# A Mamba and mixture-of-experts layer on one core: expert features spread over the partitions by copies, one DMA per routing weight tile, and a planner with free buffers and one DMA queue

## The chip, the core and the metric

The kernel runs on one core of one Trainium2 chip. The metric is device time in microseconds, the median of several runs. The core has TensorE (PE, matrix products), VectorE (DVE), ScalarE (ACT), GpSimd (POOL) and SyncE (SP, which here issues DMAs). Each engine executes its own queue of instructions in order and waits on semaphores for the others. Sixteen DMA engines move data between the device memory (DRAM) and the on-chip memories: SBUF, and PSUM, into which TensorE writes. Both have 128 partitions.

## What is computed

The input is 16 batches of 256 positions with 256 features, all in 32-bit floats. Each is normalised, and two branches read the result; the output is the input plus both.

```python
xn = layernorm(x)
# branch 1: a selective state space (Mamba) layer, E = 512 features, N = 16 states
hidden, gate = split(xn @ W_in)                  # 256 -> 2 * 512
hidden = silu(causal_conv4(hidden) + conv_bias)
dt, Bm, Cm = split(hidden @ W_x, [128, 144])
dts = softplus(dt @ W_dt + b_dt)
dA  = exp(dts[..., None] * -exp(A_log))          # 512 x 16 per position
dBu = dts[..., None] * Bm[:, :, None, :] * hidden[..., None]
state = dA * state + dBu ; y = sum_n state * Cm  # a scan over the 256 positions
out1 = ((y + hidden * D) * silu(gate)) @ W_out
# branch 2: 32 experts of 96 features each, the best 8 of a token weighted
probs = softmax(xn @ router_w.T); w = top8(probs) / sum(top8(probs))
out2 = sum_e ((silu(xn @ w_gate[e]) * (xn @ w_up[e])) @ w_down[e]) * w[:, e]
x + out1 + out2
```

All 32 experts are computed for every token; an expert that is not among a token's eight has weight zero.

## The kernel before

The work is cut into steps (small functions such as `project`, `feed`, `scan`), each on one engine. At the end of `mamba_moe_kernel` every step of every batch is handed to a planner with `add(...)` (from line 816): its engine, a length, a due time, the steps it `needs`, the buffers it `takes` and those it `gives` back. `Plan.order` (line 56) plays all of it through once at build time: whenever an engine is free, the ready step with the earliest due time starts. The order found is the order in which the instructions are issued; nothing is reordered on the chip. A due time is a base (`ORIGIN + PERIOD * b` for the Mamba steps, `ORIGIN + RATE * b + LEAD` for the experts) plus an offset per kind of step from the table `DUE`, and from `FIRST`, `SECOND` and `LAST` for the first, second and last batch. `EARLY` says how long ahead of its due time a step may start. Many offsets are thousands of microseconds, so they act as fixed ranks between kinds of steps.

Buffers of a kind form a ring of a size from `RINGS` (line 260). `open` (line 49) lets a step start when the next buffer in turn is free, and `take` (line 266) hands the buffers out strictly in turn. A DMA is modelled as a length on its issuing engine and a fixed time `lands` until its data is there; transfers do not delay one another in the model.

**Mamba branch.** `load_x`, `stats`, `root`, `invert`, `center` (two POOL instructions, line 403) and `norm` normalise; `turn` and `keep_turned` transpose to `xnT`. `project` (line 556, bank kinds g and u), `conv_first` and `conv_rest`, and `activate` make `hs`; `params`, `lift`, `turn_steps`, `widen`, `steps` make `dts`; `send_params` writes Bm and Cm to DRAM (`bcd`). `inputs` (POOL) multiplies. Then come 8 groups of 2 states: `fetch` (SP, line 680) reads two rows of B and C repeated to all partitions into `rep`; `feed` (POOL, line 692) multiplies the scan's input; `decay` (ACT), `scan` and `read` (DVE) follow, and `collect` (POOL) adds the products into `y` by an accumulating DMA. `fold`, `gated` and `project_out` end the branch; `gate` and `gate_silu` make its gate.

**Expert branch.** The 32 x 96 = 3072 features are 24 chunks of 128, in 4 parts of 8 experts or 6 chunks. `load_experts` (line 323) brings the weights of a part once, at the start, and all batches use them. `route`, `largest`, `expo` and `choose` compute the routing weights, `send_weights` writes them to DRAM (`wd`). For each part, `spread` (line 492) reads them back so that partition p of chunk c holds the weight of the expert that this feature belongs to: as 96 does not divide 128, an expert's features straddle chunks, and a part takes six DMAs (line 501) into a tile `wr` of 128 x 6 x 256. For each pair q of chunks, `gates` and `ups` (line 508, L515) are matmuls, `silu` (L528) gives `sg`, `weigh` (POOL, L534) multiplies `sg` by `wr`, `combine` (DVE, L538) multiplies by the ups to `h`, and `down` (L550) accumulates into `acc`. `settle` and `finish` add the two branches to the reloaded input, and `store` writes it.

**Opening.** ACT issues five small loads of per-feature vectors into `small` (line 291), SP the larger ones. `warm` and `keep_warm` (line 372) are transposes of the identity on TensorE whose results are not used.

## Time and profile before

| | |
|---|---|
| median of 3 runs | 1309.12 us (1308.93 to 1309.49) |
| profiled execution | 1305.62 us |
| its span, first to last instruction | 1303.3 us |
| mean granted TensorE clock | 0.992 of full speed |
| instructions | 19008 |
| DMA moved | 268.80 MB, mean 206 GB/s |
| DMA issues of `rep` / `wr` / `y` from `pr` | 128 / 384 / 222 |
| median issue to landing of these | 6.7 / 6.0 to 6.4 / 7.2 us |

The page gives each engine's busy time and its share of the span, the span in 40 slices, the DMA queues, the chain of work that ended last, and groups of instructions by source line. "PE ... L515" is an instruction of TensorE that line 515 issued; "pg<-xnT,wg_sb" names what it writes and reads; `<-` ahead of an engine's name says who ended a wait. SPq and POOLq are the engines' queues, where a DMA is issued. A batch appears in the trace as one `ph` (project) pair, 24 chunks of `pg`, `pu` and `acc`, and 16 units of `bu`, `da` and `pr`.

### The profile page before, as it was taken

The numbers are of one execution on the slowest core, as the hardware profiler recorded it, in microseconds if no ns is written. First come the engines' busy times: TensorE is split into PE (matmuls) and PEld (weight loads), VectorE is DVE, ScalarE is ACT, GpSimd is POOL, SyncE is SP. The second block draws the span as 40 slices with busy tenths as digits, with TensorE's granted clock in tenths as the row PEclk, the third lists the DMA queues.
The fourth block names the chain that finished last, engine by engine and source line by source line (L and its number), as shares of the span: only waits on it lengthen the run. The fifth ranks groups of instructions, "written<-read, shape, count | busy, mean of one in ns | idle before, by whom it ended". The sixth has DMA issues, their size and how long they took to land.

```text
span 1303.3 us, 19008 instructions
## 1 busy us (share of the span) xinstructions
PE 1269.5 (97%) x6010; PEld 1111.8 (85%) x6010; DVE 1157.6 (89%) x1735; ACT 1102.1 (85%) x1888; POOL 1181.3 (91%) x835
## 2 busy tenths in 40 slices
PE   8988999999999999999999999999999999999998
PEld 7877788888888888888888888888888888888877
DVE  3778899999899999998989999889989899889887
ACT  5869898998889989798897989799888898888873
POOL 1778999999999999999999999989999899898994
PEclk8998999999999999999999999999999999999999
DMA  9999999998999989899998999989899898989994
GB/s 248 245 225 204 194 221 210 222 209 184 219 218 213 217 195 213 195 219 196 203 221 192 211 208 207 211 199 213 190 208 206 195 234 185 210 191 204 204 228 83
DMA packets 174292, 268.80 MB, mean 206 GB/s; under 512 B 42704, under 2 KB 108272, under 8 KB 174192
## 3 DMA queue, kind: packets, MB, share of 16 engines
q0 software_dynamic: 36576, 124.80, 50.8%
q1 hardware_dynamic: 134976, 142.75, 41.0%
q8 instruction: 47, 0.77, 0.2%
q10 hardware_dynamic: 2640, 0.05, 0.1%
q14 instruction: 53, 0.43, 0.1%
HBM read 137.51 MB, written 5.24 MB: 110 GB/s over the span
## 4 chain that ended last, share of the span: by engine, by line
PE 56%; POOL 19%; DMA 7%; issue 6%; ACT 6%; DVE 5%; SPq 1%; POOLq 0%; DVEq 0%; ACTq 0%
PE acc L550 15%; PE pu L515 14%; PE pg L515 14%; POOL bu L695 7%; POOL sg L534 5%; POOL y L734 4%; PE po L788 3%; DMA wr<-wd 3%; PE ph L561 3%; PE pgate L762 3%; DMA rep<-bcd 2%; ACT da L709 2%; PE px L599 2%; DVE da L717 2%; PE pdt L643 1%
## 5 line engine op out<-in xcount | busy, mean ns | idle before, releaser
L695 POOL TENSOR_TENSOR bu<-rep,hs 128x1024 f32<-128x1024 f32 x256 | 701.0, 2893 | 39.8 <-DVE da L717 20.0
L717 DVE TENSOR_TENSOR_SCAN da<-da,bu 128x512 f32<-128x512 f32 x512 | 608.8, 1216 | 38.4 <-ACT da L709 25.9
L709 ACT ACTIVATE da<-dts,a_sb 128x256 f32<-128x256 f32 x1024 | 469.2, 473 | 95.4 <-DVE pr L729 71.7
L550 PE MATMUL acc<-wd_sb,h 128*128 128x256 f32 x1536 | 364.8, 380 | 5.3 <-DVE h L538 4.8
L515 PE MATMUL pu<-xnT,wu_sb 128*128 128x256 f32 x1536 | 360.0, 380 | 7.5 <-DVE h L538 6.4
L515 PE MATMUL pg<-xnT,wg_sb 128*128 128x256 f32 x1536 | 350.1, 381 | 6.3 <-ACT sg L528 5.6
L515 PEld LDWEIGHTS pg<-xnT,wg_sb 128*128 128x128 f32 x1536 | 292.7, 191 | 48.5 <-ACT sg L528 6.8
L515 PEld LDWEIGHTS pu<-xnT,wu_sb 128*128 128x128 f32 x1536 | 290.4, 191 | 48.9 <-DVE h L538 8.5
L550 PEld LDWEIGHTS acc<-wd_sb,h 128*128 128x128 f32 x1536 | 291.6, 191 | 46.9 <-DVE h L538 6.7
L534 POOL TENSOR_TENSOR sg<-sg,wr 128x512 f32<-128x512 f32 x192 | 317.8, 1858 | 4.9 <-DMA wr<-wd 3.4
L734 POOL DMA_DIRECT2D y<-pr x222 | 289.3, 1313 | 23.0 <-DVE da L717 6.1
L729 DVE TENSOR_TENSOR pr<-da,rep 128x512 f32<-128x512 f32 x448 | 293.4, 675 | 5.4 <-issue 2.9
L538 DVE TENSOR_TENSOR h<-pu,sg 128x512 f32<-128x512 f32 x192 | 130.9, 682 | 61.9 <-POOL sg L534 36.6
L709 ACT ACT_TABLE_LOAD x135 | 173.2, 1283 | 2.4
L528 ACT ACTIVATE sg<-pg 128x512 f32<-128x512 f32 x192 | 104.7, 593 | 4.1 <-PE pg L515 1.7
L528 ACT ACT_TABLE_LOAD x81 | 103.9, 1283 | 3.5 <-PE pg L515 2.2
L584 DVE SCALAR_TENSOR_TENSOR hs<-ph,small,hs 128x255 f32<-128x255 f32 (+2 forms) x192 | 76.8, 471 | 2.9 <-ACT hs L573 2.9
L753 POOL TENSOR_TENSOR y<-y 128x512 f32<-128x512 f32 x32 | 67.6, 2233 | 2.2 <-DMA y<-pr 2.2
L561 PE MATMUL ph<-xnT,win_sb 128*128 128x256 f32 x256 | 64.1, 396 | 1.9 <-DMA win_sb<-in_L_attn_W_in_dram 1.9
L788 PE MATMUL po<-wout_sb,y 128*128 128x256 f32 x256 | 62.1, 386 | 2.9 <-POOL y L778 2.9
L762 PE MATMUL pgate<-xnT,win_sb 128*128 128x256 f32 x256 | 58.2, 380 | 2.0 <-ACT sg L528 1.9
L778 POOL TENSOR_TENSOR y<-y,gs 128x512 f32<-128x512 f32 x30 | 58.4, 2414 | 0.0
(69 smaller groups left out, 844.9 us busy)
## 6 DMA issues: line engine op xcount, KB each, us to landing
y<-pr POOLq DMA_DIRECT2D x222, 512.0 KB, 7.2
rep<-bcd SPq DMA_DIRECT2D x128, 512.0 KB, 6.7
wr<-wd SPq DMA_DIRECT2D x128, 192.0 KB, 6.0
wr<-wd SPq DMA_DIRECT2D x128, 128.0 KB, 6.4
wr<-wd SPq DMA_DIRECT2D x128, 64.0 KB, 6.0
y<-sk POOLq DMA_DIRECT2D x32, 256.0 KB, 7.2
xt<-L_attn_input_states_dram SPq DMA_DIRECT2D x16, 256.0 KB, 6.0
o<-L_attn_input_states_dram SPq DMA_DIRECT2D x16, 256.0 KB, 6.5
```

Of the source, the lines that this page charges most:

```text
L515: nc.tensor.matmul(p[:, j, :], w[:, hc, ts(c, P)], xs[:, hc, :], start=(hc == 0), stop=(hc == HC - 1),)
L528: nc.scalar.activation(sg, live.pop(("g", b, q)), AF.Silu)
L534: nc.gpsimd.tensor_mul(sg, sg, wr[:, r : r + 2, :])
L538: nc.vector.tensor_mul(h, live.pop(("u", b, q)), live.pop(("sg", b, q)))
L550: nc.tensor.matmul(acc[:, s, :], h[:, j, ts(s, P)], wd_sb[:, c, :], start=(c == 0 and s == 0), stop=(c == FC - 1), skip_group_check=True,)
L561: nc.tensor.matmul(ph[:, j, :], win_sb[:, hc, ts(2 * q + j, P)], xs[:, hc, :], start=(hc == 0), stop=(hc == HC - 1),)
L695: nc.gpsimd.tensor_mul(bu, live["rep", b, g][:, 0:1].to_broadcast([P, CPU, NG, L]), live["hs", b][:, ts(u, CPU), :].unsqueeze(2).to_broadc ...
L709: nc.scalar.activation(da[:, i, :], dts[:, c, :], AF.Exp, scale=a_sb[:, c, n : n + 1])
L717: nc.vector.tensor_tensor_scan(flat, flat, live["bu", k][:, j].rearrange("p n l -> p (n l)"), 0.0, op0=ALU.mult, op1=ALU.add,)
L729: nc.vector.tensor_mul(live["pr", k][:, :, j, :], live.pop(("da", m)), live["rep", b, g][:, 1])
L734: nc.gpsimd.dma_start(live["y", b, u].rearrange("p n c l -> p (n c l)"), live.pop(("pr", k)).rearrange("p n c l -> p (n c l)"), accum_op=A ...
L788: nc.tensor.matmul(po[:, s, :], y[:, 0, j, ts(s, P)], wout_sb[:, c, :], start=(c == 0 and s == 0), stop=(c == EC - 1), skip_group_check=True,)
```

## The change

Features are laid out anew. A part of 8 experts has 768 features; partition p now holds features 6p to 6p + 5 of the part, so 16 partitions hold one expert and all six chunks of a part have the same expert on a given partition. A routing weight tile is then 128 x 256, loaded by one DMA, and `weigh` reads it for both chunks of a pair. The down weights come in this order from one DMA of whole rows per part. Gate and up weights are loaded by the same kind of DMA as before, into one of four staging areas (the second buffers of `y0`, `y1`, `hs`, `dts`, which batch 1 is the first to use), and a VectorE copy `deal` puts them in the new order; 16 loads and 16 copies. The second batch's `project` needs the last copy.

The planner gives a step any free buffer, the one longest free (`spare`), instead of the next in turn; it keeps steps of one kind in order; it models one DMA queue through which all transfers pass one after another, and at most 8 outstanding transfers of SP. Rings: `wr` 4 for 2, `sg` 5 for 3, `h` 3 for 2. `gates` and `gate` are two steps each in place of one, with a lock that keeps a pair together. `down`-weight loads are steps of their own. The small loads are issued by POOL instead of ACT, the first batch's `center` is one VectorE instruction, its `route` comes after its first `project`, and `keep_warm` makes 20 and 8 transposes in place of 6 and 4. All offsets in the tables are new, and ORIGIN, PERIOD, RATE and LEAD are -27.68, 78.24, 79.23 and -62.04, for -13.55, 77.76, 77.96 and -22.78.

```diff
 class Plan:
+    BEGIN = dict(SP=1.3, POOL=2.0)
+    FINISH = 0.6
+    LANES = 8
...
-    def open(self, ring, count):
...
+    def transfer(self, st, now):
+        piece = st["length"] / st["parts"]
+        for _ in range(st["parts"]):
+            if st["engine"] == "SP":
+                now = max(now, self.lanes.pop(0))
+            self.busy = max(self.busy, now + self.BEGIN[st["engine"]]) + st["moves"] / st["parts"]
+            landed = self.busy + self.FINISH
+            if st["engine"] == "SP":
+                self.lanes.append(landed)
+            now += piece
+        return now, landed
+
+    def spare(self, ring):
+        return [
+            k for _, k in sorted(
+                (self.given[key], k) for k, key in enumerate(self.slots[ring]) if key in self.given
+            )
+        ]
...
-        rep=3, bu=3, pr=4, da=AHEAD, g=2, u=2, acc=1, wr=2, sg=3, h=2, gs=2, o=1,
+        rep=3, bu=3, pr=4, da=AHEAD, g=2, u=2, acc=1, stage=4, pair=1, wr=4, sg=5, h=3, gs=2, o=1,
...
-        i = taken[ring] % RINGS[ring]
-        taken[ring] += 1
+        i = plan.homes[ring].pop(0)
...
-        nc.scalar.dma_start(
+        nc.gpsimd.dma_start(
             small[:, :, 0:KC], conv_k.rearrange("(c p) o k -> p c (o k)", p=P)
...
+    STAGES = ("y0_1", "y1_1", "hs_1", "dts_1")
+
+    def load_down(j):
+        nc.sync.dma_start(
+            wd_sb[:, ts(j, CPG), :],
+            w_down[ts(j, EPG)].rearrange("e i h -> (e i) h").rearrange("(p c) h -> p c h", c=CPG),
+        )
+
+    def load_experts(j, kind, hc):
+        src = {"g": w_gate, "u": w_up}[kind]
+        home = STAGES[plan.homes["stage"].pop(0)]
+        stage = sb.tile([P, SLAB], F32, tag=home, name=f"stage_{j}_{kind}_{hc}")
+        stage = stage[:, : EPG * I].rearrange("p (e i) -> p e i", e=EPG)
+        nc.sync.dma_start(stage, src[ts(j, EPG), ts(hc, P), :].rearrange("e p i -> p e i"))
+        live["stage", j, kind, hc] = stage
+
+    def deal(j, kind, hc):
+        dst = {"g": wg_sb, "u": wu_sb}[kind]
+        stage = live.pop(("stage", j, kind, hc)).rearrange("p e i -> p (e i)")
+        nc.vector.tensor_copy(
+            dst[:, hc, ts(j, CPG), :], stage.rearrange("p (m c) -> p c m", c=CPG)
+        )
...
     def center(b):
+        if b == 0:
+            nc.vector.scalar_tensor_tensor(
+                nmr, mv[:, :, 0:1], -1.0, rstd, op0=ALU.mult, op1=ALU.mult
+            )
...
     def spread(b, g):
-        wr = take(sb, "wr", [P, CPG, L], f"wr_{b}_{g}")
-        half = EPG // 2
-        for e in range(half):
-            lo, hi = e * I, (e + 1) * I
-            while lo < hi:
-                c, r = divmod(lo, P)
-                n = min(hi - lo, P - r)
-                nc.sync.dma_start(
-                    wr[r : r + n, c :: CPG // 2, :],
-                    wd[g * EPG + e : (g + 1) * EPG : half, :].partition_broadcast(n),
-                )
-                lo += n
+        wr = take(sb, "wr", [P, L], f"wr_{b}_{g}")
+        rows = live["wd", b][ts(g, EPG), :]
+        nc.sync.dma_start(wr, rows.unsqueeze(1).to_broadcast([EPG, ROWS, L]))
...
     def weigh(b, q):
-        nc.gpsimd.tensor_mul(sg, sg, wr[:, r : r + 2, :])
+        sg, wr = live["sg", b, q], live["wr", b, 2 * q // CPG]
+        nc.gpsimd.tensor_mul(sg, sg, wr.unsqueeze(1).to_broadcast([P, 2, L]))
...
-    add("keep_warm", (1,), "PE", 1.3, -490.0, 6, needs=[("turn_router",)])
-    add("keep_warm", (2,), "PE", 0.8, -490.0, 4, needs=[("turn", 0)], gives=["warm"])
+    add("keep_warm", (1,), "PE", 2.3, -490.0, 20, needs=[("turn_router",)])
+    add("keep_warm", (2,), "PE", 0.9, -490.0, 8, needs=[("turn", 0)], gives=["warm"])
...
+            for hc in range(HC):
+                add("load_experts", (j, kind, hc), "SP", 0.6, due, j, kind, hc, moves=1.65,
+                    takes=[("stage", ("stage", j, kind, hc))])
+                add("deal", (j, kind, hc), "DVE", 0.85, due, j, kind, hc,
+                    needs=[("load_experts", j, kind, hc)], gives=[("stage", j, kind, hc)])
...
+        dealt = [("deal", PARTS - 1, "u", HC - 1)] if b == 1 else []
```

The offsets that set SP's first issues are, by kind, `DUE` plus `FIRST`: `load_again` -7024.7 - 13951.6, `load_x` -8639.1 + 792.8, `load_in` 1119.4 - 7928.7, `load_router` -358.6 - 6402.5, `load_steps` -7426.2 + 5634.6, `load_experts` -3572.6 + 1952.1, `load_out` 9300.8 - 2.6. Their base times are -27.68, -210, -199 and 20, -200, -198, -89.7 and 45. `EARLY` holds the four down loads back to about 18, 38, 57 and 77 of the planner's microseconds.

## The prediction

> **What bounds the kernel now.** I read the busy shares and slices first, then busy time by stage, then TensorE's instructions in time, then the chain of waits, then the DMA queue's own waits.
>
> ```profile
> PE 1269.5 (97%) x6010; PEld 1111.8 (85%) x6010; DVE 1157.6 (89%) x1735; ACT 1102.1 (85%) x1888; POOL 1181.3 (91%) x835
> DMA  9999999998999989899998999989899898989994
> 80.00:100.00 20.00, 16.42 (x75) 13.85 (x74) 14.60 (x22) 10.46 (x21) 15.90 (x11) 0.91 0.81 215
> 100.00:180.00 80.00, 71.59 (x332) 62.06 (x331) 69.70 (x103) 69.10 (x119) 72.61 (x52) 0.96 0.95 202
> 500.00:580.00 80.00, 80.00 (x384) 70.60 (x383) 74.55 (x111) 69.78 (x121) 73.86 (x52) 1.00 0.93 205
> ```
>
> The stage rows give length, then busy us of PE, PEld, DVE, ACT and POOL, then granted clock and DMA share. From 500 to 580 TensorE never stops: here it is the bound. Sixteen matmuls start over 3.45 us, 0.216 us each, and the same step of two batches (686.82 and 764.79 in the chain) lies 77.97 us apart. Sixteen batches are 16 x 77.97 = 1247.5 us of work that the change leaves alone, so only what TensorE loses can be won: 1303.3 - 1247.5 = 55.8 us. POOL has 1181.3 / 16 = 73.8 us a batch, DVE 72.4, ACT 68.9: little room when one of them is late.
>
> ```profile
> 8.45 1.08 PE L438 MATMUL pl<-rwT,xnT 128*128 128x32 f32 x8 [0.24 <-ACT xnT L428]
> 11.44 6.20 PE L561 MATMUL ph<-xnT,win_sb 128*128 128x256 f32 x16 [1.91 <-DMA win_sb<-in_L_attn_W_in_dram]
> 87.11 2.75 PE L550 MATMUL acc<-wd_sb,h 128*128 128x256 f32 x8 [3.16 <-DVE h L538]
> 110.86 6.00 PE L515 MATMUL pg<-xnT,wg_sb 128*128 128x256 f32 x16 [5.34 <-ACT sg L528]
> 137.62 1.99 PE L515 MATMUL pu<-xnT,wu_sb 128*128 128x256 f32 x8 [3.05 <-DVE h L538]
> ```
>
> Each row is start, length, instructions, and in brackets the idle time before it. Setting each stretch of matmuls against 0.216 us apiece gives the losses: (a) 12.8 us up to 17.47, of 17.47 us only 4.7 being work (turn 0.44, routing 0.82, project 3.45); (b) 18.5 us from there to 140: 1.7 before 28.2; 3.3, 0.6, 5.5 and 3.2 idle; and 0.8 + 1.0 + 2.4 because matmuls after the 3.16 and 5.34 us gaps ran at a granted clock of 0.50 for some 4 us; (c) 16.4 us after 140, in 17 pieces of 0.4 to 2.3, nearly 13 of them after 860; (d) 3.9 us behind the last matmul. The rest, some 4 us, is in gaps under 0.35.
>
> ```profile
> 0.74 3.22 DMA small<-_L_attn_conv_kernel_dram
> 3.98 0.37 SPq L795
> 5.46 5.84 DMA win_sb<-in_L_attn_W_in_dram
> ...
> 62.38 1.31 POOL sg L534
> 63.69 1.80 SPq L501
> 66.72 9.80 DMA wr<-wd
> 76.68 1.27 POOL sg L534
> ...
> 314.74 9.36 DMA wr<-wd
> 324.17 6.72 DMA rep<-bcd
> ```
>
> The chain (start, length, what) says why. At the start SP stands still from 2.15 until ACT's `small` load has landed, so `win_sb` is issued only at 5.46. Later, a routing weight tile comes free (`weigh`, L534), SP writes out its six DMAs (L501), they land 9.8 us later, POOL waits, and VectorE and TensorE after it: the idle at 84 to 87 follows. The same pair stands at 314, before the 1.3 us loss at 346. SP's own waits say the same:
>
> ```profile
> SPq L501 <- POOL sg L534: 129.0, 32, 10.4
> SPq L683 <- DVE pr L729: 306.4, 81, 11.1
> ```
>
> What waits behind a `wr` DMA on SP are the `rep` fetches (L683) that `feed` needs.
>
> **The change, part by part.**
>
> *Routing weights.* Now 384 DMAs (L501, median 0.599 us of SP each) carry 64 x 128 x 6 x 1 KB = 50.3 MB. After: 64 DMAs, 8.4 MB. SP is freed of 320 x 0.6 = 192 us, 12 a batch. The queue's kind carries 142.75 MB in 41.0% of the engines' time, so 41.9 MB are about 12% of it, and the mean DMA share falls from 0.93 to about 0.81. Landings (`wr` 6.1, `rep` 6.7, `y` 7.2 us median) should shorten, I take by a tenth to a quarter. `weigh` reads one row for both chunks; no POOL row has just that, but `feed` reads both operands repeated at 2.33 us for 1024 (2.28 ns each) against `weigh`'s 1.26 for 512 (2.46), so I cost it at nothing, between -0.1 and +0.1 us each, and +0.1 x 12 = 1.2 a batch stays inside POOL's 4.2 of room.
> The Trainium skill speaks against the new form: "DMA: Bandwidth & Descriptors", section Rules for kernel authors, says that an outermost dimension below 16 confines a transfer to that many engines, and this source's outermost dimension is 8. No row here shows such a transfer. By it 128 KB would take 8 engines about 1.0 us instead of 0.5 at the first slice's 248 GB/s, an estimate; the sum would not move, since four tiles give most of a batch of lead.
>
> *Deeper buffers, any free one:* `wr` 4 for 2, `sg` 5 for 3, `h` 3 for 2. This is what lets a late transfer pass: one `sg` more holds 1.73 us of matmuls, two 3.5, against stalls of 0.4 to 5.5. TensorE's order, with `gates` and `gate` split into halves of 1.73 us, can fill more holes.
>
> *Opening.* SP takes what is due first. Base time plus the tables give -21004 for the residual (256 KB), -8056 for x (256), -7008 and -6789 for the halves of `win_sb` (512 each), -6961 for the router (32). Before, x alone landed at 3.83: 0.74 for the issue, 256 KB at 248 GB/s is 1.06, so 2.0 fixed. After: x at about 4.9, `win_sb` 7.0, router 7.1 (before 4.5). From x to the turned x took 8.40 - 3.83 = 4.6 us; `center` on VectorE, one instruction of 0.2 instead of POOL's 0.62 from invert to norm, takes 0.3 off. Turned x is then due at 9.1; but the router's turn at 7.1 and the 20 identity turns behind it stand ahead on TensorE's queue if they are ready first: 20 x 0.11 (rate of the four turns at 7.61) ends at 9.7, 20 x 0.23 (rate of the first fourteen) at 12.1. So `project` starts between 9.1 and 13.3, likeliest 11, against 11.44, and takes 3.45 or 6.2. Routing (0.82) now follows it. Gain on (a): from 4.1 (9.1, full clock) to -2.9 (13.3, half); at 11 it is +2.2 at full clock, -0.5 at half, and I take +1.
> On the clock, the rows first: granted 0.50 from about 9.9 to 16.5, after small matmuls and a 1.91 gap; and turns that started 0.23 apart ran 0.11 apart from 7.6 on, so turns alone came to full speed. The skill's "TensorE: Matmul & The Clock Gate", Part 4, says that transposes do not count as activity for the clock the way matmuls do. By the page `project` would again take 6.2, and the gain be -0.5.
>
> *Per-feature loads on POOL.* Five DMAs of 512 pieces each. POOL's rows are 0.84 to 1.3 us for 128 pieces: 5 x 0.84 = 4.2 us at least, 5 x 4 x 1.3 = 26 at most. POOL's first work is at 27.05, so nothing is lost up to there, though `conv_first` could wait for the second load: 1.4 + 2 x 5.2 + 4 = 16 at worst, its old start 15.2. I take 0, range 0 to 5. ACT sheds five issues and SP the 1.83 us wait.
>
> *Sixteen copies on VectorE* of 768 elements. The trace has no such copy. `conv_rest` takes 0.47 for 255 elements, `read` 0.675 for 512: by the slope 0.88 for 768, between 0.47 (no longer than the short one) and 1.01 (the rate of the long one). I take 0.88, the slope of the two nearest: 16 x 0.88 = 14 us. VectorE is busy 11.6 of the first 40 us: hidden, unless a copy waits for its load; then everything behind it on VectorE (`conv_rest`, `combine`, the scans) waits too. Bytes ahead of load n of 16: 2.19 MB + 0.39 n, with `wout_sb`, two of the late down loads and routing between; at 248 GB/s the first lands near 13, the last copy ends near 48, and batch 1's `project` (36.69 before) goes there. Its `inputs` came at 117.65, and batch 0 needed 40.45 - 11.44 = 29 us for that path: 48 + 29 = 77, covered by 40. TensorE meanwhile has gate, 5 `sg` of gates, two ups and params: 3.45 + 8.6 + 3.45 + 2.17 = 17.7 us while weights arrive. Cost nothing, range 0 to 15.
>
> *Sum.* (b): the 9.8 us `wr` event and the four stalls after it; of 18.5 I take 12 back (range 0 to 17). (c): 16.4, mostly behind `wr` and `rep`; I take 9 back (range 0 to 15). (a) +1, (d) 0. 1305.62 - 22 = 1283.6 for a profiled run (2.3 us beyond its span); the median shown is 3.5 above the profiled run: **1287**.
>
> **Rivals.** *Clean:* TensorE hardly stops after the opening: 4 + 16 + 14 = 34, time 1275. For it: 400 to 560 runs so already. Against: POOL keeps 73.8 of 78, and VectorE 72.4.
> *The fetches were not the cause:* POOL's order and its lack of room are; transfers get shorter and POOL just waits elsewhere, as at 1000 to 1006 where TensorE waits on `gated` behind a `y` DMA of 10.57 us, which the change leaves as it is. Then 1 + 6 + 0 = 7: 1302.
> *Slower, the copies hold VectorE:* rounds of four loads land late, copies block VectorE, and TensorE loses what it lost behind the late `wr` (3.16 idle + 1.8 slow = 5) in each of four rounds, 20, with the 9 of (c) kept: 1309 + 20 - 9 = 1320. It decides once a round lands more than about 5 us behind its place (9.8 late cost 5). Against: the loads' median landing was 6.0 and 5.4 us amid twelve spread DMAs.
> *It does not do what it says:* a new order that plays out much as the old, no change: 1309.
>
> **How the numbers follow.** Forecast 0.48 (own range 1279 to 1295), clean 0.17, not the cause 0.22, no change 0.03, slower 0.10. A change under 0.2% (2.6 us) can't be told from none. Faster 0.48 + 0.17 + 0.22 = 0.87, same 0.03, slower 0.10. Low end 1270, the clean case with 5 more; high end 1308, just short of the slower case; some 0.05 and 0.12 left out.
>
> **What would show it.** 64 `wr` issues and a DMA share near 0.81; no SP wait at 2; `project` at 9 to 13; no TensorE gap over 2 us between 20 and 140; fewer pieces after 860; VectorE's copies done by 50 with no wait over 2 us before one. I am wrong if TensorE's gaps stay with `wr` landing early, or if copies head the list of VectorE's waits.

## The result and the profile after

The change made the kernel slower: 1324.61 us (median of 4 runs, 1322.03 to 1330.53) against 1309.03 for the kernel before beside it, a ratio of 1.0134 [1.0091, 1.0177]. The profiled execution took 1326.04 us, its span 1324.3, at a mean granted clock of 0.996. The forecast was 1287.

The page first: engine lines and the DMA share in 40 slices.

```profile
PE 1274.1 (96%) x6028; PEld 1111.0 (84%) x6028; DVE 1178.3 (89%) x1752; ACT 1121.5 (85%) x1905; POOL 1187.6 (90%) x838
DMA  9687687886987868698796978879697896968885
```

The transfers shrank as they were meant to (226.80 MB, 64 issues of `wr`). TensorE's busy time rose by 4.6 us and its span by 21.0, so most of the difference is idle time. Two of the stages shown before (length, busy us of PE, PEld, DVE, ACT, POOL, granted clock, DMA share, GB/s):

```profile
100.00:180.00 80.00, 74.26 (x354) 64.71 (x353) 71.24 (x100) 69.17 (x121) 69.09 (x48) 0.98 0.74 154
500.00:580.00 80.00, 77.68 (x369) 67.52 (x368) 73.02 (x110) 69.73 (x121) 73.50 (x53) 1.00 0.80 167
```

From 500 to 580 TensorE never stopped before, at 384 matmuls; now it does 369 and stands 2.3 us, with DMA engines, VectorE, ScalarE and GpSimd all no busier than they were. Its instructions in time show where (in brackets the idle time ahead, and who ended it):

```profile
14.93 1.97 PE L599 MATMUL ph<-xnT,win_sb 128*128 128x256 f32 x8
...
68.41 5.17 PE L558 MATMUL pg<-xnT,wg_sb 128*128 128x256 f32 x16 [5.39 <-ACT sg L567]
...
167.09 3.59 PE L825 MATMUL po<-wout_sb,y 128*128 128x256 f32 x8 [2.50 <-DVE h L576]
...
291.62 1.99 PE L588 MATMUL acc<-wd_sb,h 128*128 128x256 f32 x8 [3.05 <-DVE o L837]
...
457.32 3.53 PE L588 MATMUL acc<-wd_sb,h 128*128 128x256 f32 x8 [2.84 <-DVE h L576]
```

The rows of the kernel before stand in the prediction: `project` starts at 14.93, not 11.44; and there are now stops of 2.5 to 3 us after 140, where the kernel before had none over 2.3. The chain of waits shows what the one at 457 is made of (start, length, what):

```profile
437.16 0.24 DVE wT L530
...
440.06 4.80 DMA wd<-wT
...
444.95 10.11 DMA wr<-wd
...
455.19 1.27 POOL sg L572
...
456.48 0.70 DVE h L576
457.32 3.53 PE acc L588 x8
```

The routing weights are chosen at 437.4, written to DRAM, read back, and 17.8 us later the first `weigh` of the batch has them, while its `gates` are long done. How far routing runs ahead has changed. The fourth batch's `route` (`pl`), first `wr` issue and first `gates` (`pg`), in the kernel before and then in the changed one:

```profile
215.97 0.97 PE L438 MATMUL pl<-rwT,xnT 128*128 128x32 f32 x8
...
250.28 4.76 SPq L501 DMA_DIRECT2D wr<-wd  x6
...
261.43 3.62 PE L515 MATMUL pg<-xnT,wg_sb 128*128 128x256 f32 x16
```

```profile
264.63 0.97 PE L492 MATMUL pl<-rwT,xnT 128*128 128x32 f32 x8
...
267.25 1.89 PE L558 MATMUL pg<-xnT,wg_sb 128*128 128x256 f32 x8
...
275.79 3.57 SPq L549 DMA_DIRECT2D wr<-wd  x4
```

Before, `route` came 45 us and the `wr` issue 11 us ahead of the batch's first `gates`; now `route` comes 2.6 us ahead of them and the `wr` issue 8.5 us behind. In batches 2 to 14 the lead of `route` was 38 to 62 us and is 2.6 to 2.8. The waits say it in sum (us in total, times, longest):

```profile
DVE h L576 <- POOL sg L572: 44.9, 16, 5.9
POOL sg L572 <- DMA wr<-wd: 34.0, 9, 11.5
DVE wg_sb L369 <- DMA stage_g<-in_L_ffn_w_gate_dram: 18.2, 3, 9.4
```

GpSimd waited for `wr` 3.4 us before; it is 34.0 now, with a sixth of the bytes (8.4 MB for 50.3). One wait of 11.5 us in the opening (up to 39.4) is part of that; 22.5 us come behind it.

**TensorE's loss** is the measure used from here on: the time up to a point less 0.216 us for each 256-column matmul done by then (narrower ones by their own rate); "end" is the end of the last matmul. Up to five points, in us:

| kernel | 20 | 140 | 740 | 1260 | end |
|---|---|---|---|---|---|
| before | 12.8 | 31.6 | 36.8 | 52.1 | 54.2 |
| after | 14.6 | 33.5 | 56.5 | 67.0 | 74.7 |
| 1 old weights, new order | 14.9 | 33.8 | 58.2 | 60.6 | 67.8 |
| 2 old order, one DMA | 11.4 | 23.5 | 25.7 | 35.6 | 35.8 |
| 3 old order, new layout | 14.9 | 45.9 | 54.8 | 61.9 | 64.0 |
| 5 old order, stride of six | 12.4 | 28.0 | 40.3 | 52.3 | 54.9 |
| 10 new order, no copies | 14.4 | 23.0 | 46.9 | 61.9 | 69.6 |
| 11 the same, three waits removed | 12.7 | 24.4 | 47.3 | 53.4 | 58.5 |
| 17 old order, stride of three | 12.9 | 28.2 | 33.4 | 47.6 | 48.0 |

After equals before up to 140 (+1.9) and loses 41.2 us behind that where before loses 22.6.

### The profile page after: what moved, and what is told of

Read it like the earlier page. It is cut to its first block, busy times and chain, and to the rows that moved or that the text cites. A ratio compares the mean times of both kernels' runs of the same rounds, so it can differ in the third digit from the quotient of the medians.

```text
span 1324.3 us, 18511 instructions
## 1 busy us (share of the span) xinstructions
PE 1274.1 (96%) x6028; PEld 1111.0 (84%) x6028; DVE 1178.3 (89%) x1752; ACT 1121.5 (85%) x1905; POOL 1187.6 (90%) x838
## 2 busy tenths in 40 slices
DMA packets 122656, 226.80 MB, mean 171 GB/s; under 512 B 34560, under 2 KB 56112, under 8 KB 122560
## 3 DMA queue, kind: packets, MB, share of 16 engines
q0 software_dynamic: 36736, 124.84, 50.3%
## 4 chain that ended last, share of the span: by engine, by line
PE 27%; ACT 22%; DVE 14%; POOL 14%; DMA 12%; issue 8%; SPq 2%; POOLq 0%; ACTq 0%; DVEq 0%
ACT da L747 8%; PE acc L588 7%; PE pg L558 7%; PE pu L558 7%; POOL bu L733 5%; DVE da L755 5%; DMA y<-pr 5%; ACT L747 4%; POOL sg L572 4%; DMA wr<-wd 3%; POOL y L772 3%; DMA wd<-wT 3%; DVE hs L622 3%; DVE pr L767 2%; PE ph L599 2%
## 5 line engine op out<-in xcount | busy, mean ns | idle before, releaser
L733 POOL TENSOR_TENSOR bu<-rep,hs 128x1024 f32<-128x1024 f32 x256 | 724.5, 3023 | 13.2 <-DVE da L755 7.4
L558 PE MATMUL pg<-xnT,wg_sb 128*128 128x256 f32 x1536 | 357.5, 381 | 11.0 <-ACT sg L567 7.2
L772 POOL DMA_DIRECT2D y<-pr x222 | 306.8, 1383 | 33.1 <-DVE pr L767 10.8
L791 POOL TENSOR_TENSOR y<-y 128x512 f32<-128x512 f32 x32 | 61.3, 2144 | 9.1 <-DMA y<-pr 9.1
L599 PE MATMUL ph<-xnT,win_sb 128*128 128x256 f32 x256 | 61.1, 381 | 3.2 <-ACT sg L567 3.2
L825 PEld LDWEIGHTS po<-wout_sb,y 128*128 128x128 f32 x256 | 48.6, 194 | 13.4 <-DVE h L576 2.9
```

Of the source, the lines that this page charges most:

```text
L558: nc.tensor.matmul(p[:, j, :], w[:, hc, 2 * q + j, :], xs[:, hc, :], start=(hc == 0), stop=(hc == HC - 1),)
L733: nc.gpsimd.tensor_mul(bu, live["rep", b, g][:, 0:1].to_broadcast([P, CPU, NG, L]), live["hs", b][:, ts(u, CPU), :].unsqueeze(2).to_broadc ...
L772: nc.gpsimd.dma_start(live["y", b, u].rearrange("p n c l -> p (n c l)"), live.pop(("pr", k)).rearrange("p n c l -> p (n c l)"), accum_op=A ...
L825: nc.tensor.matmul(po[:, s, :], y[:, 0, j, ts(s, P)], wout_sb[:, c, :], start=(c == 0 and s == 0), stop=(c == EC - 1), skip_group_check=True,)
```

## The experiments

The rival theories at the start: O, the new order puts steps, routing above all, too late for what they feed; L, the new small transfers are themselves slow; C, the copies hold VectorE.

### 1 to 4: transfers, order, layout, model

**1.** The changed kernel; each batch uses the routing weights of the one before, so that none waits for its own.

```diff
-        rows = live["wd", b][ts(g, EPG), :]
+        rows = live["wd", max(b - 1, 0)][ts(g, EPG), :]
```

> The changed kernel, instruction for instruction, except that each routing weight tile from the second batch on is read from the batch before (its weights are one batch old; the round trip of this batch's weights through DRAM is left out of what POOL waits for). Theory O (the new order puts routing too late for the trip choose, write, read back): POOL's waits on wr (34.0 us, 9 times) shrink to the opening's 11.5, the batch period between 700 and 1100 falls from 79.4 towards 78.2, time 1306 to 1316. Rival L (the new transfers themselves cost, or other places of the order): period stays at 79 and time at 1320 or more.

Measured 1318.39 (1313.47 to 1321.78), ratio 1.0095 [1.006, 1.013]: 6.2 below the changed kernel, between the two expectations. GpSimd's wait for `wr` behind the opening fell from 22.5 to 1.9 us (in the opening it stands just as long, 11.4 us), and from 740 to 1260 TensorE lost 2.4 us in place of 10.5; the stops before 740 stayed. The late round trip is real, and less than half of the 15.6 us to be explained.

**2.** The kernel before, its planner and order untouched, with one DMA per `wr` tile; the weights stay as they were, so the regrouping is left out.

```diff
-        wr = take(sb, "wr", [P, CPG, L], f"wr_{b}_{g}")
...
+        wr = take(sb, "wr", [P, L], f"wr_{b}_{g}")
+        rows = live["wd", b][ts(g, EPG), :]
+        nc.sync.dma_start(wr, rows.unsqueeze(1).to_broadcast([EPG, P // EPG, L]))
...
```

> The kernel before, its order and planner untouched, with the routing weight tile as 128 x 256 and one DMA in place of six; the expert weights stay in their old layout, so the regrouping of features is left out. Theory O: the smaller transfer only helps, 1290 to 1304, DMA share near 0.81. Rival L: one DMA per tile lands late, POOL waits on wr grow past the 3.4 us of before, time 1309 or more.

Measured 1289.22 (1286.76 to 1290.94), ratio 0.9879 [0.9848, 0.991]. Its stages:

```profile
100.00:180.00 80.00, 73.66 (x345) 64.49 (x346) 72.73 (x108) 71.25 (x122) 75.35 (x56) 0.98 0.84 177
500.00:580.00 80.00, 79.63 (x381) 69.97 (x380) 73.94 (x111) 69.90 (x120) 74.65 (x54) 1.00 0.81 176
```

The DMA share from 500 to 580 is 0.81 as in the changed kernel, and TensorE stands 0.4 us there, not 2.3. So L falls: the transfers are worth 17.5 us, and the changed kernel doesn't get them.

**3.** The second, with the new layout: staged loads and 16 copies, each ahead of the first use of its part.

```diff
+                nc.vector.tensor_copy(
+                    dst[:, hc, ts(n[0], CPG), :], st.rearrange("p (m c) -> p c m", c=CPG)
+                )
...
```

> The kernel before with the whole new layout (staged expert loads, sixteen VectorE copies placed just ahead of the first matmul that needs them or of the load that reuses their stage, one DMA per weight tile) in the old order with the old planner. Theory O: within 8 us of e2, 1290 to 1308. Rival C (the copies hold VectorE and TensorE in the opening): 15 us or more above e2, with gaps of TensorE before 80 us.

Measured 1316.81 (1315.16 to 1317.59), ratio 1.0084 [1.0058, 1.0111]: 27.6 above the second, all of it lost before 180 us. One such stop (VectorE's instructions, then TensorE's):

```profile
94.77 9.48 DVE L333 COPY wu_sb<-stage_u 128x768 f32<-128x768 f32 x2
...
103.64 3.58 PE L531 MATMUL pu<-xnT,wu_sb 128*128 128x256 f32 x8 [7.86 <-DVE wu_sb L333]
```

Two copies that take 0.85 each elsewhere last 9.48 us. C holds for this order, by a mechanism that experiments 9 to 16 look for.

**4.** The changed kernel, its planner counting 2.5 us more for the landing of `send_weights` and `spread`.

```diff
-            landed = self.busy + self.FINISH
+            landed = self.busy + self.FINISH + self.LATE.get(st["name"][0], 0.0)
```

> The changed kernel whose planner counts 2.5 us more for the landing of send_weights and of spread; tables unchanged, so the whole order is found anew. Theory O: routing moves earlier, POOL's waits on wr fall below 15 us in all, time 1305 to 1318. If any new order is as good or bad as the last (the tables suit one model only): 1318 to 1335.

Measured 1473.53 (1473.35 to 1479.83), ratio 1.1298 [1.1262, 1.1334]. The planner's own total for this model is 1448.4 us, and 1283.3, 1283.8 and 1293.8 for 0, 0.5 and 1.0 us more. The due tables serve one model only; the old planner finds no complete order at all with 0.5 us more in `lands` of the same two steps. New tables for the old planner, or old ones for the new, were not tried, so what in the new order is worse, the rule or the tables, stays open.

### 5 to 8: a layout without copies, the opening, deeper buffers

**5.** The second with the whole layout and no copies: the matmul's weights are every sixth column of the part as it was loaded.

```diff
-                    p[:, j, :], w[:, hc, ts(c, P)], xs[:, hc, :],
+                    p[:, j, :], w[:, hc, part, :, m], xs[:, hc, :],
...
```

> The order of before and one DMA per routing weight tile, as in the second experiment, but with the new layout in full and no copies: gate and up weights stay as they were loaded, and the matmul reads every sixth column of a part as its weights; down weights come by the one DMA of whole rows. If the new order is what costs (theory O), layout and small transfers are free: 1286 to 1293 us, within 0.3% of the second experiment's 1289.2. If weights read at a stride of 24 bytes load more slowly (96 such loads a batch; a load that grew from 0.18 to 0.36 us would exceed the 0.216 us between matmuls by 0.15), 1289 + 16 x 96 x 0.15 = 1520.

Measured 1306.25 (1304.59 to 1307.51), ratio 1.0002 [0.9988, 1.0016]: 17.0 above the second, neither free nor the 230 us of the rival. TensorE never stops from 180 to 980, and yet falls behind by 0.9 us every 40. The groups of weight loads (PEld) of the second and of the fifth experiment, with busy us and mean ns of one:

```profile
L505 PEld LDWEIGHTS pg<-xnT,wg_sb 128*128 128x128 f32 x1536 | 292.3, 191 | 44.6 <-ACT sg L518 4.0 <-ACT gs L762 0.3 <-ACT hs L562 0.2
```

```profile
L507 PEld LDWEIGHTS pg<-xnT,wg_sb 128*128 128x128 f32 x1536 | 351.6, 309 | 4.8 <-ACT sg L520 3.2
```

191 against 309 ns: the stride of 24 bytes lengthens a load by 118 ns, of which 0.017 us a matmul come through (1.65 us a batch over 96 loads).

**6.** The changed kernel with its order, copies left out, weights read at the same stride.

```diff
     def deal(j, kind, hc):
+        pass
...
+                    p[:, j, :], w[:, hc, part, :, m], xs[:, hc, :],
```

> The changed kernel with its order kept, the 16 copies and their staging left out, the weights read at a stride instead. TensorE lost only 1.9 us more than in before up to 140 us, so by theory O (the order) the copies are a small part: 1312 to 1322 us. If the copies hold VectorE (rival C), as they did in the old order where they came to 27.6 us, the time falls by 15 to 28: 1297 to 1310, and it is lost nowhere later.

Measured 1329.81 (1325.73 to 1331.01), ratio 1.0178 [1.015, 1.0206]: outside both. The loss at 140 fell from 33.5 to 26.6, and more than that was lost again behind 140. It mixes two things, copies left out and a stride put in; the tenth, which has neither, takes 8.1 us less.

**7.** The changed kernel with 6 identity turns in place of 20 before the turn of x.

```diff
-        for i in range(count):
+        for i in range(6 if count == 20 else count):
```

> The changed kernel, order kept, with 6 identity turns in the place of 20 ahead of the turn of x. project starts near 11.9 instead of 14.9. Theory O: the opening is 3 us of 15, so 1319 to 1326 us. If the opening is what the rest hangs on, the gain is larger than 5 us; if the twenty turns are what brings the clock up, project takes 6.2 instead of 3.5 us and nothing is gained.

Measured 1325.77 (1319.45 to 1327.34), ratio 1.0142 [1.0102, 1.0182]. TensorE's loss at 18 fell by 1.7, but a stop of 1.90 us for `hs` at 20.4 takes that back, and the end shows none of it.

**8.** The fifth with `wr` 4, `sg` 5, `h` 3, the planner still counting 2, 3, 2: the same order.

```diff
-        ... wr=2, sg=3, h=2, gs=2, o=1,
+        ... wr=4, sg=5, h=3, gs=2, o=1,
...
+    plan = Plan(dict(RINGS, wr=2, sg=3, h=2))
```

> The fifth experiment with wr 4, sg 5 and h 3 buffers, while the planner goes on counting 2, 3 and 2: the same order, with fewer waits possible. The trace of the second experiment shows TensorE losing 2.3 us between 140 and 740 us and 12.3 after 140 in all, so there is little left to win: 1281 to 1290 us, 0 to 8 below the fifth. If buffers are what the late transfers needed, as the prediction had it, more than 8.

Measured 1305.57 (1303.02 to 1307.76), ratio 0.9995 [0.998, 1.001]: nothing.

### 9 to 11: copies made later; the new order alone

**9.** The fifth, with each slab of 768 columns copied into a spare slab behind its last use in batches 1 to 4, and read without a stride from then on.

```diff
+        nc.vector.tensor_copy(
+            slabs[to].rearrange("p (c f) -> p c f", c=CPG),
+            slabs[k].rearrange("p (f c) -> p c f", c=CPG),
+        )
...
```

> The fifth experiment (old order, one DMA per routing weight tile, weights read at a stride), with the 16 copies made later: after its last use in batches 1 to 4, each 768-column slab is copied into the one spare slab, four a batch, at most one behind each combine, and read without a stride from then on. A strided weight load took 0.309 us there, a contiguous one 0.191; TensorE lost some 1.65 us a batch by it. Left of that are 2 + 0.75 + 0.5 + 0.25 = 3.5 batches, 5.8 us; 16 copies of 0.85 us on VectorE lie in its 6 us of room a batch. So 1289 + 6 = 1295, 1291 to 1300 us. If VectorE can't take a copy without TensorE noticing (rival C), 16 x 0.85 = 14 us more: 1305 to 1312.

Measured 1320.59 (1320.43 to 1324.04), ratio 1.012 [1.0094, 1.0146]: rival C, and worse than its 14 us. By tile, with shortest, median and longest ns, the copies beside the products `pr` on the same engine:

```profile
L352 DVE COPY slab<-slab x16: 833/2656/7285, 107.0 to 458.7; 128x768 f32<-128x768 f32 x16
...
L744 DVE TENSOR_TENSOR pr<-da,rep x448: 651/676/693, 52.9 to 1301.0; 128x512 f32<-128x512 f32 x150
```

The longest copy and GpSimd's instructions beside it, in time:

```profile
112.43 7.29 DVE L352 COPY slab<-slab 128x768 f32<-128x768 f32 x1
...
112.79 2.65 POOL L710 TENSOR_TENSOR bu<-rep,hs 128x1024 f32<-128x1024 f32 x1
115.11 1.56 POOL L548 TENSOR_TENSOR sg<-sg,wr 128x512 f32<-128x512 f32 x1
116.34 2.64 POOL L710 TENSOR_TENSOR bu<-rep,hs 128x1024 f32<-128x1024 f32 x1
```

The run of GpSimd's instructions ends at 118.98, the copy at 119.72, 0.74 us later, about the time of one unhindered copy. The long copies at 158, 210, 218, 297 and 308 end 0.7 to 0.8 us behind such a run likewise; the short one at 107.04 falls into a stretch in which GpSimd only issues a DMA. The Trainium skill states the rule ("SBUF — State Buffer", sections "SBUF: two separate sides" and "Who interferes with whom"): VectorE in a two-port mode and GpSimd contend for one pair of ports, held for a whole instruction, and the loser waits. This trace agrees for copies, at up to 6.4 us of waiting; which mode a copy ran in, no row shows. The long copies of the changed kernel (at 52.0, 53.7 and 59.1) end 0.72 us behind a GpSimd instruction as well.

**10.** The changed kernel and its order, weights loaded and read as before; no staging, no copies, no stride.

```diff
-                    p[:, j, :], w[:, hc, 2 * q + j, :], xs[:, hc, :],
+                    p[:, j, :], w[:, hc, ts(c, P)], xs[:, hc, :],
```

> The changed kernel, order kept, with the gate and up weights loaded and read as before: no staging, no copies, no stride; the regrouping of the features is left out, as in the second experiment. Against the second experiment (1289.2, same transfers, same weights, old order) it differs by the new order, the deeper buffers and the opening's small parts alone. Theory O: 1310 to 1320 us. If the copies are most of the loss (rival C): 1290 to 1300.

Measured 1321.73 (1315.62 to 1327.49), ratio 1.0123 [1.0073, 1.0172]. This is the clean comparison: same work, same transfers (but for the form of the four down loads and who issues the small ones) and same weights as the second experiment, and 32.5 us more. By the table, TensorE's loss in the profiled runs is 33.8 us larger: 3.0 up to 20, 3.5 less from there to 140, 21.7 from 140 to 740, 5.1 to 1260 and 7.5 behind it. Leaving out the copies gave 10.5 us of TensorE's time up to 140 (33.5 to 23.0), and all but 2.9 us (within the intervals) was lost again behind that, with the waits for `sg` as long as ever:

```profile
DVE h L575 <- POOL sg L571: 45.1, 16, 7.6
...
POOL sg L571 <- DMA wr<-wd: 21.2, 9, 3.9
```

**11.** The tenth, with routing weights one batch old, a second buffer for `o`, and 6 identity turns.

```diff
-        for i in range(count):
+        for i in range(6 if count == 20 else count):
...
-        rows = live["wd", b][ts(g, EPG), :]
+        rows = live["wd", max(b - 1, 0)][ts(g, EPG), :]
...
-        o = take(sb, "o", [P, SPS, H], f"o_{b}")
+        o = sb.tile([P, SPS, H], F32, tag=f"o_{b % 2}", name=f"o_{b}")
```

> The tenth with three named waits taken away and the order kept: routing weights one batch old (so none waits for its round trip), a second buffer for the reloaded input o, and 6 identity turns in place of 20. If these waits are how the new order costs its time (theory O as now put: routing late, 7 us; o behind the store, 5; the turns, 2): 14 below the tenth, 1296 to 1306. If the order costs by many small waits everywhere, no more than 8 below it.

Measured 1316.75 (1305.1 to 1320.82, a wide spread; the profiled execution, span 1308.4, is among the short ones), ratio 1.006 [1.003, 1.0089]. 5.0 below the tenth: the second expectation. Behind the opening GpSimd waits for `wr` 2.2 us, once. Of the stops behind `o` one goes and one stays in spite of the second buffer, because there VectorE waits for the reload itself:

```profile
281.14 0.69 DVE L836 TENSOR_TENSOR o<-acc,o 128x512 f32<-128x512 f32 x1 [3.50 <-DMA o<-L_attn_input_states_dram]
```

27.5 us against the second experiment remain, in many stops of 0.3 to 2.6 us, some behind ScalarE (`sg`, `xt`, `dts`), some behind VectorE (`h`, `hs`, `o`). Most lie between 140 and 740, where experiments 1, 10 and 11 lose 24.4, 23.9 and 22.9 us and the second loses 2.2; from 740 to 1260 experiment 1 loses no more than 2.4.

One more view bears on them: when a batch's `route` starts on the chip, less when the planner's own clock has it start (us):

| batch | 1 | 3 | 6 | 9 | 12 | 16 |
|---|---|---|---|---|---|---|
| before | -2.8 | 2.2 | 1.3 | -0.1 | -0.5 | 7.3 |
| 2 old order, one DMA | -2.8 | -5.9 | -9.2 | -11.4 | -11.7 | -11.0 |
| after | 0.5 | 13.2 | 17.8 | 25.8 | 28.4 | 33.1 |
| 10 new order, no copies | 0.3 | 2.8 | 8.2 | 16.0 | 19.6 | 28.4 |

The old plan ends at 1295.8 us; its fixed landing times (5.5 to 8 us for these transfers) fit the crowded queue, and with small transfers the chip runs ahead of it. The new plan promises 1283.3, with transfers that land 0.6 us behind the queue and a `wd` trip that took 4.80 and 10.11 us at 440. In the new plan's own clock TensorE stands 5.8 us between 140 and 740, so most of what the chip loses there is not in the plan. The chip falls behind it from the third batch on, without the copies too, and it never catches up. That its order is too tight for the chip is what this table suggests; it is not shown apart from the tables' other effects.

### 12 to 16: why copies take so long

**12.** The ninth, each copy written as a maximum of the slab with itself (two operands).

```diff
-        nc.vector.tensor_copy(
+        nc.vector.tensor_max(slabs[to].rearrange("p (c f) -> p c f", c=CPG), src, src)
```

> The ninth, with each late copy made as the maximum of the slab with itself in place of a plain copy. There a plain copy took 0.84 to 7.29 us, mean 2.83, and ended when a run of GpSimd instructions ended; products of two SBUF operands (pr from da and rep, 0.675 us for 512) show no such spread. If a plain copy has to wait for GpSimd and a two-operand instruction does not (theory G), each takes 0.9 to 1.0 us and the time is what the ninth was expected to be, 1291 to 1300. If VectorE has no room for 16 x 0.95 us at all (rival C), it stays at 1310 to 1320.

Measured 1333.58 (1328.67 to 1335.2), ratio 1.0204 [1.0181, 1.0227]; 3.63 us each.

```profile
L353 DVE TENSOR_TENSOR slab<-slab x16: 1530/3380/7275, 107.8 to 472.0; 128x768 f32<-128x768 f32 x16
```

This form takes 1.53 us where nothing holds it, the copy 0.83; beyond that the 16 wait some 34 us in all, the copies some 32. So it waits as the copy does, and the added time is its own length. The comparison that led here was not of like with like: `pr` is no instruction with two operands in SBUF, as its `da` lies in PSUM (taken from the pool `ps`).

**13.** The same exchange in the third.

```diff
-                nc.vector.tensor_copy(
+                nc.vector.tensor_max(dst[:, hc, ts(n[0], CPG), :], st, st)
```

> The third experiment (old order, new layout, copies in the first batch), with the same exchange of the copy. There 16 copies took 29.7 us instead of 13.6, the longest pair 9.48, and TensorE lost 27.6 us to the second experiment up to 180 us. Theory G: the copies take 15 us and 10 to 25 of the 27.6 go: 1292 to 1307. If late loads and copies as such are what costs (rival C): 1311 to 1318.

Measured 1324.63 (1323.08 to 1325.07), ratio 1.0142 [1.0126, 1.0159]; 2.10 us each for the gate weights and 2.90 for the up weights, the shortest 1.50. The escape that theory G offered falls.

**14.** The twelfth with the small loads on GpSimd and the first `center` on VectorE.

```diff
-        nc.scalar.dma_start(
+        nc.gpsimd.dma_start(
```

> The twelfth with two parts of the change's opening: the small per-feature loads issued by GpSimd, and the first batch's center as one VectorE instruction. SP no longer stands still behind the small loads up to 3.96 us, so win_sb and x may land 1 to 2 us sooner and project start so much earlier: 0 to 2 us below the twelfth. If the prediction's worst case holds (conv_first waits for the small loads), up to 5 above.

Measured 1333.99 (1332.74 to 1339.89), ratio 1.0222 [1.0197, 1.0247]: the twelfth's time. These two parts neither gain nor cost.

**15.** The ninth with its copies on ScalarE, at the same points.

```diff
-        nc.vector.tensor_copy(
+        nc.scalar.copy(
```

> The ninth, with the 16 late copies on ScalarE, issued at the same points. ScalarE copies 512 elements in 0.58 us and passes over 1024 in 1.06, so 768 take some 0.82, 13 us in all, and it has 11 us of room a batch in the second experiment. If a VectorE copy stands waiting while GpSimd works (theory G, which the two-operand form did not escape), ScalarE's take 0.8 each, and the time is what the ninth was expected to be: 1291 to 1300 us. If it is the place of the copies, or the rewriting of weights that TensorE reads, that costs: 1310 to 1335.

Measured 1304.27 (1302.16 to 1306.52), ratio 0.9985 [0.9972, 0.9999], 16.3 below the ninth, though each copy takes longer than a free VectorE copy:

```profile
L352 ACT COPY slab<-slab x16: 1563/1594/1629, 107.7 to 442.1; 128x768 f32<-128x768 f32 x16
```

1563 to 1629 ns with no spread: ScalarE doesn't wait for GpSimd. The same copies at the same points in the same order, so place and rewriting are not what cost the ninth its time; the engine is. At twice the length that was expected, they still cost: TensorE lost 14.4 us from 140 to 500, and at most 5.8 for the stride of the first batches and 1.0 that the second experiment lost there leave 8 or more.

**16.** The ninth, source walked in its own order, written at a stride.

```diff
-            slabs[to].rearrange("p (c f) -> p c f", c=CPG),
-            slabs[k].rearrange("p (f c) -> p c f", c=CPG),
+            slabs[to].rearrange("p (c f) -> p f c", c=CPG),
+            slabs[k].rearrange("p (f c) -> p f c", c=CPG),
```

> The ninth, with the same copies on VectorE walking the source in its own order and writing at a stride instead of reading at a stride. If the read at a stride of 24 bytes is what makes VectorE's copy wait for GpSimd, the 16 take 0.8 to 1.0 us each and the time falls to 1291 to 1300. If a copy as such waits (theory G), they take 2 to 4 us again and the time stays at 1315 to 1335.

Measured 1323.63 (1321.94 to 1324.99), ratio 1.0126 [1.0104, 1.0149]; 0.973 to 7.398 us. The stride of the read is not the reason.

### 17 and 18: a version that beats both

**17.** The fifth with three features to a partition: four experts share three chunks, the weight load reads every third column, and a part has two `wr` DMAs.

```diff
-            part, m = divmod(2 * q + j, CPG)
+            part, m = divmod(2 * q + j, CPG // 2)
...
+        wr = take(sb, "wr", [P, 2, L], f"wr_{b}_{g}")
+        half = EPG // 2
+        for s in range(2):
+            rows = live["wd", b][ts(2 * g + s, half), :]
+            nc.sync.dma_start(wr[:, s, :], rows.unsqueeze(1).to_broadcast([half, P // half, L]))
```

> The fifth experiment (old order, no copies, weights read at a stride where they were loaded) with three features to a partition in place of six: four experts share three chunks, 32 partitions each. The weight load then reads every third column (12 bytes apart, not 24), and a part's routing weights are a tile of 128 x 2 x 256 from two DMAs of 128 KB. In the fifth a load took 0.309 us against 0.191 without a stride, and TensorE lost 1.65 us a batch. If the extra time grows with the stride, a load takes some 0.24 and the loss is less than half, 0 to 12 us in all; 64 more DMAs cost SP 0.6 x 4 = 2.4 us a batch of what it was freed of, 0 to 3 us. So 1289 to 1301 us, likeliest 1293: faster than both kernels. If any stride costs the same, 1306 to 1309.

Measured 1297.73 (1296.03 to 1301.17), ratio 0.9934 [0.9912, 0.9956]: 8.1 us faster than the kernel before beside it and some 27 faster than the changed one, with nothing left out.

```profile
L509 PEld LDWEIGHTS pg<-xnT,wg_sb 128*128 128x128 f32 x1536 | 336.0, 252 | 9.5 <-ACT sg L522 7.2 <-ACT gs L769 0.2
```

At 252 ns a load TensorE loses 5.2 us from 140 to 740, against 12.3 at 309 and 2.2 at 191. The price grows with the stride.

**18.** The seventeenth with `wr` 3, `sg` 5, `h` 3, the order kept.

```diff
-        ... wr=2, sg=3, h=2, gs=2, o=1,
+        ... wr=3, sg=5, h=3, gs=2, o=1,
...
```

> The seventeenth with wr 3, sg 5 and h 3 buffers while the planner goes on counting 2, 3 and 2, so that the order is the same and only waits for a free buffer can go. In the eighth experiment this changed nothing (1305.6 to 1306.3), but there TensorE was held by its weight loads throughout; here it is not. TensorE stops 5.8 us at 107 and 2.8 at 134, behind sg and h, and loses 13 us from 940 to the end. If deeper buffers let a late transfer pass, as the prediction had it: 1287 to 1294 us. If the order, not the buffers, decides: within 2 us of 1297.7, since a step issued in the old order meets no free buffer earlier than that order asks for it.

Measured 1300.03 (1296.14 to 1301.79), ratio 0.9944 [0.9922, 0.9966]: no gain again, with weight loads (252 ns) that hold TensorE less than the fifth's.

## Why the prediction was wrong

The sum predicted a profiled run of 1283.6 and it took 1326.04, 42.4 more. By its own terms: (a) opening, +1 gained against 1.8 lost: 2.8. (b) 20 to 140, 12 gained against none (18.8 lost before, 18.9 after): 12. (c) behind 140, 9 gained against 18.6 more lost (22.6 before, 41.2 after): 27.6.

**What bounds the kernel** and **routing weights** held. The second experiment, which is this part alone, won 17.5 us, and the DMA share came to 0.80 (from 500 to 580) for 0.81; `y` landed in 6.5 us for 7.2.

**The step that failed** is term (c), "I take 9 back (range 0 to 15)", with what it rests on: that deeper buffers and split gates "let a late transfer pass" and "can fill more holes". It took the new offsets, a complete reordering of every engine, at nothing, since the page has no row for an order. The order by itself costs 32.5 us (experiment 10 against 2, with the deeper buffers and the opening in it, which by 7, 8, 14 and 18 count for next to nothing). Of it the late routing is 6 us in the changed kernel (experiment 1), that with `o` and the turns 5 in the tenth (experiment 11); the rest is many small stops, most of them between 140 and 740, whose common cause is open. The deeper buffers are worth nothing in the old order (8 and 18): a step asks for a buffer when the order says so. What the diff did show, and I passed over, is that `gates` now need `route`, and that `route` ranks behind `gates` in the tables (offsets 637.9 against -30.2, where they were -99.0 against -26.3), so that it comes just ahead of them; the trip from `choose` to `weigh` was there to be priced.

**Term (b)** failed by the copies, "Cost nothing, range 0 to 15". In the changed kernel they took 10.5 us of TensorE's time up to 140 (experiment 10), about what should have been gained there. Their length was right while GpSimd was idle (0.82 to 0.88), the last ended at 60, not 48, and waits of 8.16 and 9.44 us stood ahead of two. The wait of 9.44 us is for a load, the case that the prediction named ("unless a copy waits for its load") and counted as covered; the stop of 5.39 us at 68.41 follows it and the four copies behind it. Not priced at all was that a copy waits for GpSimd. In the changed kernel that is a small part, as most copies come when GpSimd has little to do: 17.2 us in all for 16, some 3.6 more than 16 free ones, against 29.7 in the third.

**The opening.** x landed at 4.42 (4.9 predicted), the router at 9.2 (7.1), and the 20 turns behind it ran 0.21 us apart, so `project` came at 14.93, past the bound of 13.3; it then ran at full rate, 1.80 us for its first 8 matmuls. The 6.2 us that the prediction held possible behind turns did not come: the clock was granted in full at 13.34, with nothing but turns on TensorE before it. The seventh experiment shows that it made no difference at the end. The small loads on GpSimd cost 0, as predicted (14).

**The rivals.** "Slower, the copies hold VectorE" gave 1320, near the result, but by another account: its four stops of 5 us in the first batch are one of 5.4 (the copies took 10.5 us in all there, not 20), and without copies the kernel is within 2.9 us of what it was. "The fetches were not the cause" falls by the second experiment: where the order stays, they were. None of the rivals was that the new order itself is worse.

## What to carry to other kernels

A hand-ranked order is a part of the change with a price of its own: try the other parts in the old order first, and compare the planner's clock with the chip's. Routing that goes out to DRAM and back needs some 18 us ahead of its first use here, and freed bytes don't buy that. A layout that needs copies can be had by reading at a stride instead, and of the two strides tried here the smaller is the cheaper.

## What the runs showed of the hardware

A VectorE copy from SBUF to SBUF waits while GpSimd works: 0.833 to 7.285 us for the same 768 elements, where ScalarE takes 1.563 to 1.629. The page of the Trainium skill named above ("SBUF — State Buffer", section "SBUF: two separate sides") counts VectorE's instructions with two SBUF operands among those that contend with GpSimd. These runs agree: the maximum of a slab with itself waited (3.63 us on average, 1.53 when nothing held it), while the products `pr`, whose `da` lies in PSUM and only `rep` in SBUF, took 0.651 to 0.693 us in all 448 cases, beside a GpSimd that is busy nine tenths of the time.

A weight load of 128 x 128 in 32-bit floats took 191 ns from adjacent columns, 252 at 12 bytes and 309 at 24; matmuls 0.216 us apart hide most of that, not all. In the changed kernel turns alone ran 0.21 us apart from 9.2 to 13.4 and 0.11 apart behind that; the first granted clock in this trace is 1.0, at 13.34.
